# Weight blocks fetched two products ahead, and three second norms one product sooner, in a four-stage layer chain on one core

## The chip, the cores and the metric

The kernel runs on one core of one Trainium2 chip. The metric is device time in microseconds (us) of one execution; the numbers below are medians of several executions. Everything is float32. In the profile PE is the matmul engine, PEld its weight load, DVE the vector engine, ACT the activation engine, POOL the GpSimd engine and SP the engine that issues most transfers. The profile writes two records for each matmul of this kernel, so "x16" is eight matmuls.

## The reference

Input x has 4 batches of 1024 tokens with 1024 features. Four stages follow each other, each closed by a residual sum and a layer norm without weights:

```python
x = _layernorm(x + _L0_attn_ref(x, weight, mask))       # x @ (weight * block mask).T
x = _layernorm(x + _L0_ffn_ref(x, ...))                 # x @ W.T + bias, + a LoRA term for some batches
x = _layernorm(x + _L1_attn_ref(x, ...))                # the sequence model, below
x = _layernorm(x + _L1_ffn_ref(x, ...))                 # x @ W.T + b, + 8 routed LoRA experts per batch
```

The sequence model projects 1024 features to 128, runs four layers, and projects back to 1024. One layer on h (tokens by 128):

```python
y = silu(layernorm(h, l1w, l1b))       # the first norm
y = sconv(y, ...)                      # a complex first-order recurrence along the tokens, real part
h = h + y * scl                        # the linear part
y = layernorm(h, l2w, l2b)             # the second norm
y = silu(y @ w1.T + b1) @ w2.T + b2    # 128 -> 512 -> 128
h = h + y
```

## The kernel before, in words

**Units and products.** The 4096 tokens are 8 units of 512 (two for each batch). Each unit goes through stage 0 (masked attention weight), stage 1 (LoRA layer) and later stage 3. The batch's own sequence model (stage 2) is woven in between products of other units. Features lie on the 128 partitions. Stages 0 and 1 use a Strassen scheme with seven half-size products, in two halves of the output, so `project` runs 14 products (p, i) for a stage: `weight(p, i)` gives the operand, eight matmuls of 128x256 into one of four PSUM banks (`mm`), an eviction on DVE (z<-mm,z) or, for i = 0, on ACT, and then `tick()`. One product with its pieces is one tick of a clock.

**The blocks.** From unit 1 on, the seven combined weight blocks come from device memory: `a0q_s` for stage 0, `a1q_s[b]` for stage 1 (one for each batch, with that batch's LoRA term merged in). `streamed(q)` returns a `weight` that takes a tile "wq" (128 x 4 x 256, 512 KB) from a pool of five buffers and issues its load on SP (L420) at that product. A load can start once PE has finished with the buffer's earlier block. `adapt1(b)` merges the LoRA weights in pieces planned at ticks around the unit before their use, and stores the blocks of `a1q_s[b]` on SP (L301). On the same queue stand the next unit's input xT (`load_x`, L472, two loads of 1 MB), reloads x<-x_s for the sequence model's way out (`leave`, L583), reloads w<-a_s for the merges (L845), the sequence model's tables ct and sn (L872) and layer weights mw (L876). SP issues its transfers in one order; each also waits until the transfer eight places earlier has landed.

**Who sets the order.** PE and DVE are reached through `InOrder` (L83 to L110), which keeps their instructions in the program's order; so all their lines show as L104 in the profile. ACT, POOL and SP instructions are ordered by the framework, from the program's order and from when it reckons that operands and buffers are ready.

**The plan.** `put(at, piece, pe, dve)` hangs a piece of side work on a tick; `tick()` runs what hangs there. `put_in` spreads pieces over a stretch, by the PE and DVE time that `put` has counted for its ticks. `later_rows` places a stage norm's sums on the first tick that isn't in `taken`, and sequence norms enter `taken` through `put_rows`.

**The sequence model.** `sequence(b, at, layer, ahead)` starts at tick 56b + 59. A batch's 1024 tokens are two halves j = 0, 1 of 512, the second 7 ticks behind the first; a layer takes 13 ticks for batches 0 to 2 (`slack` is then 1) and 12 for batch 3. For one layer l and half j, with `base` its first tick:

- base: `rows`: four small matmuls stats<-csq over the squares, a square root on ACT (sd, L243), a reciprocal on DVE, four broadcasts on POOL (L249) into crs. The tile sd has one buffer for the sequence.
- base + 1: `first`: crs<-h,crs on DVE, Silu on ACT. base + 2, base + 3: `scan`, two recurrences on DVE. base + 4: `joined`, three DVE products, result u.
- base + 5 + slack: `convolved`: one matmul cv<-u,csc on PE, h<-h,cv on DVE, the square csq<-h on ACT (L862).
- base + 7 + slack: `rows` again, for the second norm; base + 8 + slack: `normed`, crs<-h,crs on DVE.
- base + 9, 10, 11 + slack: `forward` in three steps: matmuls a_ps<-crs,mw, Silu on ACT (a_sb, L931), matmuls o<-a_sb,mw one step later, then h<-o,b2c,h on DVE and the next square.

The `a_ps` and `cv` results share two PSUM banks.

Of the kernel before, what the change touches and what calls it, by code (L numbers as in the profile page):

```python
# [17 lines left out]
P = 128  # L18
# [17 lines left out]
NU = NB * S // U  # L36
PRODUCT = 3.7
HU = U // 2
# [15 lines left out]
def block_kernel(  # L54
# [25 lines left out]
    nc = tc.nc  # L80
# [114 lines left out]
    def block(name, shape):  # L195
        return big(name, shape, "blk", 5)
# [60 lines left out]
    SLOTS0 = (0, 5, 4, 1, 6, 2, 3)  # L257
# [74 lines left out]
    def put(at, piece, pe=0.0, dve=0.0):  # L332
        plan.setdefault(at, []).append(piece)
        count(at, pe, dve)
# [77 lines left out]
        o = [t[0][:, 0], t[0][:, 1], t[1][:, 0], t[1][:, 1]]  # L412
        return o if cs is None else [a[:, cs, :] for a in o]

    def streamed(q):


        def weight(p, i):
            w = block("wq", [P, 4, HU])
            nc.sync.dma_start(w, q[SLOTS0[i], p])  # L420
            return lambda c, o: w[:, c, ds(o * P, P)]

        return weight

    def on_chip(parts):
        def weight(p, i):
# [6 lines left out]
    def project(weight, ops, z, after, early=None, order=IN_ORDER):  # L433

        for p, i in order:
            cs = ds(2 * p, 2)
            c11, c12 = z[0][:, 0, cs, :], z[0][:, 1, cs, :]
            c21, c22 = z[1][:, 0, cs, :], z[1][:, 1, cs, :]  # L440
            w = weight(p, i)
            ps = bank().rearrange("p (o n) -> p o n", n=HU)
            for o in range(2):
                product(ps[:, o, :], lambda c: w(c, o), ops[i], 4)
            if i == 0:
                A.copy(c11, ps)
            elif i == 1:
                V.tensor_tensor(c21, ps, c11, ALU.add)
            elif i == 2:
                V.tensor_tensor(c12, ps, c21, ALU.add)  # L450
            elif i == 3:
                V.tensor_tensor(c22, ps, c12, ALU.add)
                V.tensor_tensor(c21, ps, c21, ALU.add)
            elif i == 4:
                V.tensor_tensor(c12, ps, c12, ALU.add)
            elif i == 5:
                V.tensor_tensor(c11, ps, c11, ALU.add)
            else:
                V.tensor_tensor(c21, ps, c21, ALU.add)
            if early:  # L460
                early(p, i)
            add_squares()
            if i > 4:
                after(p, i - 5)
            tick()
# [31 lines left out]
    def stage0(ops):  # L497
        ssum, z, t = big("ssum", [P, U], "ssum", 2), z_tiles(), t_tiles([4, HU])
        norm = {}

        def after(p, j):
            for c in range(2 * p, 2 * p + 2):
                square_in(z[j][:, :, c, :], None, ssum, p == 0 and j == 0 and c == 0)

        def early(p, i):
            cs = ds(2 * p, 2)
            lo, hi = ([z[j][:, h, cs, :] for h in range(2)] for j in range(2))
            for k in {4: (3,), 5: (1, 2), 6: (4,)}.get(i, ()):
                right_sum(k, lo, hi, t_out(t, cs))

        project(streamed(a0q_s), ops, z, after, early)
        later_rows(1, lambda: norm.update(rs=norm_rows(ssum)))
        return mixed(z, t), norm

# [334 lines left out]
    def sequence(b, at, layer, ahead):  # L849


        st = {}

        def h_of(j):
            return hs[b][:, ds(j * HF, HF)]

        def t_tile(name):
            return big(name, [P, HF], "t", 4)

        def square(j):  # L860
            st[j, "sq"] = sq = t_tile("csq")
            A.activation(sq, h_of(j), AF.Square)  # L862

        def rows(j):
            sd, seg = rstd_rows(st[j, "sq"], HF, avg_c, "sc")
            st[j, "y"] = rs = t_tile("crs")
            spread(rs, sd, seg)

        def tables_in(l, j):
            for k, (name, src) in enumerate((("ct", ct_s), ("sn", sn_s))):  # L870
                st[j, k] = t = big(name, [P, HF], name, 2)
                nc.sync.dma_start(t, src[l][:, ds(j * HF, HF)])  # L872

        def weights_in(l):
            st["mw"] = big("mw", [P, 2 * DFF], "mw", 1)
            nc.sync.dma_start(st["mw"], mw_s[l])  # L876

        def normed(j):
            y = st[j, "y"]
            V.tensor_tensor(y, h_of(j), y, ALU.mult)  # L880

        def first(l, j):
            normed(j)
            y = st[j, "y"]
            A.activation(y, y, AF.Silu, bias=col("ln1_b", l), scale=col("ln1_w", l))

        def scan(l, j, k):

            y = st[j, "y"]
            out = y if k else t_tile("u")  # L890
            V.tensor_tensor(out, st[j, k], y, ALU.mult)
            start = (g1i, g2i)[k][:, l : l + 1] if j == 0 else st["end", k]
            V.tensor_tensor_scan(
                out, rad[:, l : l + 1].to_broadcast([P, HF]), out, start, ALU.mult, ALU.add
            )
            if j == 0:
                st["end", k] = end = small.tile([P, 1], F32, name="end", tag=f"end{k}")
                A.copy(end, out[:, HF - 1 : HF])
            st[j, "out", k] = out

        def joined(j):
            u, y = st[j, "out", 0], st[j, "out", 1]
            V.tensor_tensor(u, st[j, 0], u, ALU.mult)
            V.tensor_tensor(y, st[j, 1], y, ALU.mult)
            V.tensor_tensor(u, u, y, ALU.add)

        def convolved(l, j):
            cv = spot("cv")
            T.matmul(cv, lhsT=csc[:, l, :], rhs=st[j, "out", 0], start=True, stop=True)
            V.tensor_tensor(h_of(j), h_of(j), cv, ALU.add)  # L910
            square(j)

        def forward(l, j, step):

            if step == 0:
                st["o"] = accp.tile([P, HF], F32, name="o2", tag="o2")
            for f in range(2 * step - 2, 2 * step):
                if f >= 0:
                    T.matmul(
                        st["o"], lhsT=st["mw"][:, ds(DFF + f * DIM, DIM)], rhs=st[f, "a"],  # L920
                        start=(f == 0), stop=(f == FC - 1),
                    )
            for f in range(2 * step, 2 * step + 2):
                if f < FC:
                    a = spot("a_ps")
                    T.matmul(
                        a, lhsT=st["mw"][:, ds(f * P, P)], rhs=st[j, "y"],
                        start=True, stop=True,
                    )
                    st[f, "a"] = s = big("a_sb", [P, HF], "a_sb", 4)  # L930
                    A.activation(s, a, AF.Silu, bias=b1c[:, l * FC + f : l * FC + f + 1])  # L931
            if step == 2:
                h = h_of(j)
                V.scalar_tensor_tensor(h, st["o"], b2c[:, l : l + 1], h, ALU.add, ALU.add)
                square(j)

        def final(j):
            V.tensor_tensor(h_of(j), h_of(j), st[j, "y"], ALU.mult)

        def put_rows(k, j):  # L940
            put(k, partial(rows, j), 0.9, 0.95)
            taken.add(k)

        slack = layer > SHORT
        for j in range(2):
            put(at + ahead * j - 1, partial(square, j))
        for l in range(DEPTH):
            for j in range(2):
                base = at + layer * l + ahead * j
                put(base - 2, partial(tables_in, l, j))  # L950
                put_rows(base, j)
                if j == 0:
                    put(base + ahead, partial(weights_in, l))
                put(base + 1, partial(first, l, j), 0.0, 0.7)
                put(base + 2, partial(scan, l, j, 0), 0.0, 1.9)
                put(base + 3, partial(scan, l, j, 1), 0.0, 1.9)
                put(base + 4, partial(joined, j), 0.0, 2.1)
                put(base + 5 + slack, partial(convolved, l, j), 0.9, 0.7)
                put_rows(base + 7 + slack, j)
                put(base + 8 + slack, partial(normed, j), 0.0, 0.7)  # L960
                put(base + 9 + slack, partial(forward, l, j, 0), 1.8, 0.0)
                put(base + 10 + slack, partial(forward, l, j, 1), 3.5, 0.0)
                put(base + 11 + slack, partial(forward, l, j, 2), 1.8, 0.75)
        for j in range(2):
            base = at + layer * DEPTH + ahead * j
            put_rows(base, j)
            put(base + 1, partial(final, j), 0.0, 0.7)
# [425 lines left out]
        put(15 + 2 * c, partial(operands0, c), 0.0, 2.8)  # L1393

    def enter(g, ops, rs):
        stage1(g, ops, rs, streamed(a1q_s[g // 2]))


    def mw_prep(l):
# [356 lines left out]
```

## Time and profile before

| what | value |
|---|---|
| median of 3 runs | 1709.11 us (1708.22 to 1710.04) |
| the profiled execution | 1708.12 us |
| its span, first to last instruction | 1706.4 us |
| mean granted TensorE clock | 0.997 |
| PE busy | 1678.1 us |
| DVE busy | 1284.9 us |
| ACT busy | 627.5 us |
| transfers, mean | 232 GB/s |

PE's matmuls are recorded in a pipeline and their ends are modelled, so a row of PE that is x16 and 3.62 long is one product of eight matmuls. The costliest groups of the page (busy time, mean ns of one, idle time just before them and what ended most of it) show what PE does:

```profile
L104 PE MATMUL mm<-tt,wq 128*128 128x256 f32 x1792 | 407.7, 381 | 0.0
L104 PE MATMUL mm<-z,wq 128*128 128x256 f32 x672 | 152.2, 380 | 2.7 <-DMA wq<-a1q_s 2.7
```

The first row reads the products that take sums of inputs, the second those that take a stage's results directly; the second has waited 2.7 us in all for blocks of stage 1.

### The profile page before, as it was taken

How to read it: one execution, taken by the hardware profiler on the slowest of the kernel's cores; microseconds unless marked ns; L12 is line 12 of the kernel's file. 1: busy time of each engine (PE TensorE's matmuls, PEld its weight loads, DVE VectorE, ACT ScalarE, POOL GpSimd, SP SyncE). 2: the span in 40 equal slices, each digit the busy share in tenths (PEclk: the TensorE clock that was granted, in tenths of full speed). 3: DMA queues.
4: the chain of work that ended last, by engine and by line, in shares of the span. 5: the costliest groups of instructions: out<-in, count | busy, mean ns of one | idle time of the engine just before them, and what ended most of it. 6: DMA issues, size and time to landing. Idle time of an engine off the chain costs nothing.

```text
span 1706.4 us, 19199 instructions
## 1 busy us (share of the span) xinstructions
PE 1678.1 (98%) x6345; PEld 1043.0 (61%) x6345; DVE 1284.9 (75%) x2173; ACT 627.5 (37%) x1079; POOL 220.3 (13%) x454
## 2 busy tenths in 40 slices
PE   7999999999999999999999999999999999999998
PEld 3488887767677666666766676765444444444444
DVE  5799889677567879767887887777778878676743
ACT  4411112355343245443333444423344642333012
POOL 1110111221011012101120111101111200100000
PEclk9999999999999999999999999999999999999999
DMA  9967879956745985576889558696536737964211
GB/s 373 367 229 268 276 259 368 358 197 222 259 136 180 324 294 172 172 284 213 297 287 340 180 167 282 223 303 211 176 111 220 227 118 246 354 221 143 94 67 62
DMA packets 194709, 395.90 MB, mean 232 GB/s; under 512 B 16657, under 2 KB 105889, under 8 KB 189874
## 3 DMA queue, kind: packets, MB, share of 16 engines
q1 hardware_dynamic: 187602, 371.82, 63.4%
q0 software_dynamic: 6048, 21.37, 3.3%
q10 hardware_dynamic: 960, 1.48, 0.2%
q8 instruction: 50, 0.82, 0.2%
q14 instruction: 49, 0.40, 0.1%
HBM read 268.39 MB, written 126.23 MB: 231 GB/s over the span
## 4 chain that ended last, share of the span: by engine, by line
PE 72%; DVE 5%; DMA 2%; ACT 0%; issue 0%; SPq 0%; POOL 0%; ACTq 0%; DVEq 0%
PE mm L104 57%; PE o L104 6%; PE a_ps L104 6%; PE stats L104 2%; DMA a1q_s<-s 1%; DVE z L104 1%; PE cv L104 1%; DVE x L104 1%; DMA wq<-a1q_s 1%; DVE u L104 1%; DVE crs L104 0%; DVE tt L104 0%; DVE w L104 0%; DVE s L104 0%; DVE ssum L104 0%
## 5 line engine op out<-in xcount | busy, mean ns | idle before, releaser
L104 PE MATMUL mm<-tt,wq 128*128 128x256 f32 x1792 | 407.7, 381 | 0.0
L104 DVE TENSOR_TENSOR z<-mm,z 128x512 f32<-128x512 f32 x339 | 226.7, 684 | 231.3 <-PE mm L104 229.8
L104 PEld LDWEIGHTS mm<-tt,wq 128*128 128x128 f32 x1792 | 337.2, 190 | 75.0 <-issue 23.7
L249 POOL PARTITION_BROADCAST crs<-sd x288 | 139.9, 595 | 825.8 <-DVE sd L104 632.0
L104 PE MATMUL mm<-w3q,x 128*128 128x512 f32 x384 | 173.0, 596 | 0.0
L104 PE MATMUL mm<-z,wq 128*128 128x256 f32 x672 | 152.2, 380 | 2.7 <-DMA wq<-a1q_s 2.7
L104 PE MATMUL mm<-xT,wq 128*128 128x256 f32 x672 | 153.1, 382 | 0.0
L104 PEld LDWEIGHTS mm<-z,wq 128*128 128x128 f32 x672 | 127.1, 190 | 33.0 <-issue 12.5
L104 PEld LDWEIGHTS mm<-xT,wq 128*128 128x128 f32 x672 | 126.1, 190 | 26.0 <-issue 6.1
L104 PE MATMUL mm<-w3q,s 128*128 128x512 f32 x288 | 130.4, 596 | 0.0
L104 PE MATMUL a_ps<-crs,mw 128*128 128x512 f32 x256 | 122.4, 601 | 5.6 <-DVE crs L104 5.6
L104 PEld LDWEIGHTS mm<-w3q,x 128*128 128x128 f32 x384 | 71.9, 190 | 88.2 <-issue 87.7
L931 ACT ACTIVATE a_sb<-a_ps,b1c 128x512 f32<-128x512 f32 x128 | 86.3, 684 | 105.0 <-PE a_ps L104 104.6
L104 DVE TENSOR_TENSOR ssum<-ssum,sq 128x512 f32<-128x512 f32 x168 | 115.5, 688 | 11.7 <-ACT sq L391 5.1
L104 DVE RECIPROCAL sd<-sd 128x128 f32<-128x128 f32 x96 | 91.1, 949 | 41.4 <-ACT sd L243 40.1
L104 PE MATMUL o<-a_sb,mw 128*128 128x512 f32 x256 | 120.3, 592 | 0.0
L691 ACT ACTIVATE sq<-z 128x512 f32<-128x512 f32 (+1 forms) x65 | 40.5, 624 | 157.4 <-DVE z L104 144.4
L104 DVE TENSOR_TENSOR w<-w,mm 128x512 f32<-128x512 f32 x128 | 81.5, 679 | 17.7 <-PE mm L104 14.2
L104 PEld LDWEIGHTS mm<-w3q,s 128*128 128x128 f32 x288 | 53.8, 190 | 65.4 <-issue 64.5
L104 PE MATMUL mm<-b,aT 16*128 16x512 f32 (+1 forms) x256 | 87.7, 620 | 0.1
L104 PEld LDWEIGHTS a_ps<-crs,mw 128*128 128x128 f32 x256 | 48.6, 192 | 59.9 <-issue 50.3
L243 ACT ACTIVATE sd<-stats,eps 128x128 f32<-128x128 f32 x96 | 35.3, 367 | 125.8 <-PE stats L104 97.2
(248 smaller groups left out, 2136.4 us busy)
## 6 DMA issues: line engine op xcount, KB each, us to landing
wq<-a0q_s SPq DMA_DIRECT2D x98, 512.0 KB, 3.4
wq<-a1q_s SPq DMA_DIRECT2D x98, 512.0 KB, 5.8
w<-a_s SPq DMA_DIRECT2D x48, 512.0 KB, 5.8
w3q<-a3q_s SPq DMA_DIRECT2D x21, 1024.0 KB, 9.8
a1q_s<-w SPq DMA_DIRECT2D x64, 256.0 KB, 3.8
x_s<-z SPq DMA_DIRECT2D x16, 1024.0 KB, 6.7
x<-x_s SPq DMA_DIRECT2D x64, 256.0 KB, 6.5
x_s<-x SPq DMA_DIRECT2D x128, 128.0 KB, 2.6
```

The costliest lines, as they stand in the source:

```text
L104: ins = op(*args, **kw)
L243: A.activation(sd[:, :seg], ps[:, :seg], AF.Sqrt, bias=eps)
L249: G.partition_broadcast(dst[:, ds(j * seg, seg)], sd[32 * j : 32 * j + 1, :seg], channels=P)
L691: A.activation(sq[:, cols], z[:, m, ds(n * HF, HF)][:, cols], AF.Square, accum_out=st[:, m, n : n + 1] if out is None else out,)
L931: A.activation(s, a, AF.Silu, bias=b1c[:, l * FC + f : l * FC + f + 1])
```

## The change

Two things, in the same functions.

First, `streamed` is no longer made for one stage. A generator lists all blocks of units 1 to 7 in order of use (stage 0's, then stage 1's, for each unit), and every call of `streamed(p, i)` issues loads until three blocks are in flight or in use (`FETCH = 2`), and then hands out the oldest. So a block's load is put into the program two products ahead of its product, also across the border between stages and units. The pool still has five buffers.

Second, for three layers (batch 0 layer 0, batch 1 layer 1, batch 2 layer 1), in the second half of the tokens, `convolved`, the second `rows` and `normed` hang one tick earlier. `forward` stays where it was.

```diff
-    def streamed(q):
-
-
-        def weight(p, i):
-            w = block("wq", [P, 4, HU])
-            nc.sync.dma_start(w, q[SLOTS0[i], p])
-            return lambda c, o: w[:, c, ds(o * P, P)]
-
-        return weight
+    FETCH = 2
+    fetched = []
+
+    def to_fetch():
+        for g in range(1, NU):
+            for q in (a0q_s, a1q_s[g // 2]):
+                for p, i in IN_ORDER:
+                    yield q[SLOTS0[i], p]
+
+    coming = to_fetch()
+
+    def streamed(p, i):
+
+        while len(fetched) <= FETCH:
+            src = next(coming, None)
+            if src is None:
+                break
+            fetched.append(block("wq", [P, 4, HU]))
+            nc.sync.dma_start(fetched[-1], src)
+        w = fetched.pop(0)
+        return lambda c, o: w[:, c, ds(o * P, P)]
...
-        project(streamed(a0q_s), ops, z, after, early)
+        project(streamed, ops, z, after, early)
...
-                put(base + 5 + slack, partial(convolved, l, j), 0.9, 0.7)
-                put_rows(base + 7 + slack, j)
-                put(base + 8 + slack, partial(normed, j), 0.0, 0.7)
+                early = slack and (b, l, j) in ((0, 0, 1), (1, 1, 1), (2, 1, 1))
+                put(base + 5 + slack - early, partial(convolved, l, j), 0.9, 0.7)
+                put_rows(base + 7 + slack - early, j)
+                put(base + 8 + slack - early, partial(normed, j), 0.0, 0.7)
...
-        stage1(g, ops, rs, streamed(a1q_s[g // 2]))
+        stage1(g, ops, rs, streamed)
```

In the program as built, PE, DVE, POOL and SP have the same number of instructions before and after, and ACT has two table loads fewer.

## The prediction

> **What bounds the kernel now.** I read the page's totals first, then the waits of PE, then the timelines around each wait, and last the chain of waits and SP's queue before them.
>
> ```profile
> PE 1678.1 (98%) x6345; PEld 1043.0 (61%) x6345; DVE 1284.9 (75%) x2173; ACT 627.5 (37%) x1079; POOL 220.3 (13%) x454
> ```
>
> PE is busy for 1678.1 of 1706.4 us, so only its idle time, about 28 us, and matmuls that run slow can be won. The waits of PE (total, times, longest) say who causes the idle time; the rest of it lies mostly at the start and the end.
>
> ```profile
> PE stats L104 <- DVE rows L104: 9.7, 2, 7.0
> PE a_ps L104 <- DVE crs L104: 5.6, 4, 2.8
> PE mm L104 <- DMA wq<-a1q_s: 2.7, 2, 2.3
> ```
>
> The change touches the second and third lines: a_ps, the first FFN matmul of a sequence layer, waiting for the normed tile crs; and stage 1's products, waiting for a weight block. PE's timeline (start, duration, idle before, releaser):
>
> ```profile
> 347.84 3.40 PE L104 MATMUL a_ps<-crs,mw 128*128 128x512 f32 x4 [2.77 <-DVE crs L104]
> 354.53 1.88 PE L104 MATMUL o<-a_sb,mw 128*128 128x512 f32 x4
> 607.81 3.69 PE L104 MATMUL mm<-z,wq 128*128 128x256 f32 x16 [0.35 <-DMA wq<-a1q_s]
> 716.53 1.98 PE L104 MATMUL a_ps<-crs,mw 128*128 128x512 f32 x4 [1.27 <-DVE crs L104]
> 735.02 0.42 PE L104 MATMUL stats<-csq,avg_c 128*32 128x128 f32 x8
> 927.98 3.69 PE L104 MATMUL mm<-z,wq 128*128 128x256 f32 x16 [2.35 <-DMA wq<-a1q_s]
> 1036.71 1.98 PE L104 MATMUL a_ps<-crs,mw 128*128 128x512 f32 x4 [1.27 <-DVE crs L104]
> ```
>
> The reader sees five places. 347.84 is batch 0, layer 0, second half; 716.53 and 1036.71 are batches 1 and 2, layer 1, second half: just the three that the change names. The four matmuls at 347.84 also take 3.40 instead of 1.98: in the table by stretches the granted clock is 0.58 from 347.8 to 351.3 and 1.00 from 351.3 on. Behind the 2.35 wait at 927.98 it is 1.00.
>
> **The sum's own time.** The profiled execution took 1708.12 (span 1706.4 and 1.72 around it), 0.99 below the median of 1709.11. Savings are worked out in that execution and taken off the median. PE's losses below are the times from start to start less the usual spacing of that kind of matmul, so they lie slightly above the gaps printed.
>
> **Part 1: second norm one product sooner, batch 0.** The loss here is 2.93 of waiting and 1.43 of matmuls at the low clock, 4.36 together. Why crs is late:
>
> ```profile
> 339.35 1.28 ACT L243 ACT_TABLE_LOAD   x1
> ```
> ```profile
> 341.05 0.95 DVE L104 RECIPROCAL sd<-sd 128x128 f32<-128x128 f32 x1 [1.97 <-ACT sd L243]
> 361.69 0.69 DVE L104 TENSOR_TENSOR z<-mm,z 128x512 f32<-128x512 f32 x1 [4.88 <-PE mm L104]
> ```
> ```profile
> 342.15 3.46 POOL L249 PARTITION_BROADCAST crs<-sd  x4 [4.40 <-PE mm L104]
> 336.50 1.26 POOL L249 PARTITION_BROADCAST crs<-sd  x4
> ```
>
> The sums end on PE at about 337.9; ACT is in a Silu and a table load until 340.6, the root ends at 341.0, the reciprocal at 342.0, four broadcasts at 345.6, the product crs<-h,crs (0.69, started at 347.10 behind two stage operations) at 347.8. In the new built order cv stands directly behind the preceding `o` matmuls (about 325.1; its operand u is ready at 319.3, so no new wait), and the four sum matmuls stand one product, 3.6, sooner (about 333.9). Two table loads fall away on ACT. Then POOL decides: it is held until 335.7 by an earlier transfer's landing and does the first half's broadcasts until 337.8; the shared small tile sd comes free only then. Root to 338.3, reciprocal to 339.4, broadcasts 1.26 (to 340.7) or, beside DVE's long operations, 3.46 (to 342.9), crs by 341.4 or 343.6. PE arrives at 344.9: the wait is gone either way, by 1.3 at least. The low clock goes with it.
>
> What is late next: the Silu results for `o`. In the new order ACT has the adapter's merge (L1229, L222) and the squares ahead of the second and third Silu; I work out their ends at about 350.4 and 352.3, while PE would want them at 350.1 and 351.0. That is a new wait of about 1.4. Net 4.36 − 1.4 = 3.0; bounds 1.0 (3.4 of new waiting: ACT's 1.28 table load and its three neighbours of 0.7 in front) and 4.36 (none). It is kept to the end: behind this place DVE idles 4.88 waiting for PE (361.69 above), so nothing there takes it back.
>
> By the Trainium skill, "TensorE: Matmul & The Clock Gate", Part 1, the array falls to half rate after an idle window of some 3.4 us. The wait here was shorter, so by the page the low clock isn't owed to it (rival D below). The row says otherwise (2.77 idle, then 0.58), and I go by the row.
>
> **Part 2: the same, batches 1 and 2.** PE's loss is 1.43 each (gap 1.27). The new crs comes at about 709.7, PE at 715.1: this wait goes. But what does PE meet next? DVE waits for PE at 707.84, and from there to 734.9 its lines leave no gap; the first and the last of them:
>
> ```profile
> 707.84 1.29 DVE L104 TENSOR_TENSOR z<-mm,z 128x512 f32<-128x512 f32 x2 [1.85 <-PE mm L104]
> ...
> 733.56 0.75 DVE L104 SCALAR_TENSOR_TENSOR h<-o,b2c,h 128x512 f32<-128x512 f32 x1
> 734.22 0.68 DVE L104 TENSOR_TENSOR h<-h,cv 128x512 f32<-128x512 f32 x1
> ```
>
> stats<-csq at 735.02 follows them through ACT's square with no printed wait. The new order has the same DVE operations in that stretch (two reciprocals of 0.95 change places, two x<-x,boutc,rs go later in it), so the chain ends where it did, and PE, 1.43 earlier, waits there. Net 0 each (bounds −0.25, a stage norm's sums and broadcasts one product later, to +1.43). Batch 2 is the same pattern, to 1055.
>
> **Part 3: blocks put into the queue two products ahead.** Most of it moves nothing: the built order of SP is the same over most of the program, because five buffers already let each load stand as early as PE frees its buffer. It differs at about seven stage boundaries, where a stage's first blocks now go ahead of the next unit's input xT, and of some stores and reloads. Only two of these have a PE wait today:
>
> ```profile
> 905.32 7.47 DMA a1q_s<-s
> 912.80 8.19 DMA a1q_s<-s
> 921.62 6.22 DMA wq<-a1q_s
> ```
>
> This is the chain of waits into 927.98: SP lets a transfer start only when the eighth before it has landed, so the block's load stands behind stores of the merged weight. In the new order the first block takes xT's place (910.7 instead of 921.6; at the other boundary 591.4 instead of 602.1), ahead of those stores. With the slowest landing in this stretch, 8.3, it is there at 919 and 600, and PE asks at 925.5 and 607.3: margins above 6. Losses 2.51 and 0.52 go, 3.03 in all (bounds 0 and 3.03). What waits behind it on SP: the last stores, four reloads x<-x_s, the second block, and xT's second half (issued some 12 later, landing about 932, first read after 940). The second block waits for a store's landing (about 921–922) and lands 7.05 later, at 929; PE, now earlier, asks at 934.2: margin about 5. At the other boundaries, and for the shifted reloads of tables and of w (one or two places), PE has no wait and consumers are 5 or more away: 0.
>
> **Sum.** 3.0 + 0 + 0.52 + 2.51 = 6.0 saved: 1708.12 − 6.0 = 1702.1 in the profiled execution, 1709.11 − 6.0 = **1703.1** as a median.
>
> **Rivals.** 0.2% is 3.42 us, about what a measurement of this kernel can tell from no change; "same" is 1705.7 to 1712.5.
> - A: DVE isn't the bound at 735 and 1055, so batches 1 and 2 keep 1.43 each: 6.0 + 2.86 gives 1700.2. For it: just before 707.84 DVE still has 1.85 to spare. Against: the 27 us without a gap behind it.
> - B: one of the two main gains fails. Either the first block stays late (its buffer or the stores hold it), 1706.1, for which the 8 us landings speak; or ACT's order eats batch 0's gain to 1.0, 1705.1, for which its 3.38 busy of 3.5 there speaks. Both together: 1709.11 − 1.0 = 1708.1.
> - C, slower: the second block holds SP. It stands at the queue's head until a store has landed, with everything behind it. If that landing and the load grew from 15.3 by more than the margin of 5 at both boundaries, PE would stand there; from about 3.0 per boundary beyond the margin the whole gain is gone, and at 5 beyond (landings near 13 each) the time is 1709.11 − 6.0 + 10 = 1713.1. For it: DMA's share is 0.97 to 1.03 from 925 to 932. Against: the bytes are the same, and a 1 MB load leaves the front of the stores.
> - D: the slow matmuls at 347.84 aren't owed to the wait, and their 1.43 stays: 1704.5. Against: both come and go together in the only two long waits shown (2.77 with, 2.35 without, which puts the threshold between them).
>
> **How the numbers follow.** Forecast 0.52 (its own range 1701.7 to 1705.1, from the new ACT wait of 0 to 3.4), A 0.16, B 0.19, C 0.09, D 0.04. Of B 0.04 lies at 1705.1, in "faster", and 0.15 in "same"; so faster is 0.52 + 0.16 + 0.04 + 0.04 = 0.76, same 0.15, slower 0.09. The range leaves out C and the edge of A and B: 1699.0 to 1709.0.
>
> **What would show it.** Right: the a_ps wait on crs shrinks from 5.6 to under 0.6 with no clock below 0.9 near 348; the wait on wq<-a1q_s vanishes; a wait of 1 to 2 appears at `o` near 350 on ACT's a_sb, and one of about 1.3 at stats<-csq where 735.02 was. Wrong: PE waits on a1q_s blocks again (the second block above all), on xT, or on z evictions behind a reordered DVE.

## The result and the profile after

The changed kernel took 1703.45 us in the median of six executions (1702.47 to 1706.05), against 1709.57 for the kernel before beside it: a ratio of 0.9965 with a 95% interval of 0.9952 to 0.9977. Run again later beside other kernels, it took 1704.43 in the median of eleven against 1708.80: 0.9974 (0.9965 to 0.9983). So it is faster by 4 to 6 us.

The profiled execution took 1704.36, with a span of 1702.6 and these waits of PE (total, times, longest):

```profile
PE stats L104 <- DVE rows L104: 9.8, 2, 7.1
PE stats L104 <- ACT csq L874: 3.4, 2, 1.7
PE stats L104 <- DVE bcol L104: 1.4, 1, 1.4
...
PE o L104 <- ACT a_sb L943: 0.9, 2, 0.7
PE a_ps L104 <- DVE crs L104: 0.3, 1, 0.3
```

The two waits that the prediction named have gone: a_ps on crs has fallen from 5.6 to 0.3, and that on wq<-a1q_s isn't in the list any more. Two new ones stand in their place, o on a_sb and stats on csq. PE's timeline at the five places (start, duration, idle before, releaser):

```profile
347.09 1.88 PE L104 MATMUL a_ps<-crs,mw 128*128 128x512 f32 x4
348.81 3.62 PE L104 MATMUL mm<-z,wq 128*128 128x256 f32 x16
352.66 1.13 PE L104 MATMUL o<-a_sb,mw 128*128 128x512 f32 x2 [0.23 <-ACT a_sb L943]
354.46 1.12 PE L104 MATMUL o<-a_sb,mw 128*128 128x512 f32 x2 [0.67 <-ACT a_sb L943]
...
606.45 3.62 PE L104 MATMUL mm<-z,wq 128*128 128x256 f32 x16
...
713.66 1.88 PE L104 MATMUL a_ps<-crs,mw 128*128 128x512 f32 x4
733.61 0.42 PE L104 MATMUL stats<-csq,avg_c 128*32 128x128 f32 x8 [1.70 <-ACT csq L874]
...
924.06 3.62 PE L104 MATMUL mm<-z,wq 128*128 128x256 f32 x16
...
1031.28 1.88 PE L104 MATMUL a_ps<-crs,mw 128*128 128x512 f32 x4
1051.23 0.43 PE L104 MATMUL stats<-csq,avg_c 128*32 128x128 f32 x8 [1.70 <-ACT csq L874]
```

And SP's, ahead of the place at 924 (start, duration, transfer):

```profile
908.93 0.33 SPq L433 DMA_DIRECT2D wq<-a1q_s  x1
909.70 0.36 SPq L301 DMA_DIRECT2D a1q_s<-s  x1
910.37 0.36 SPq L301 DMA_DIRECT2D a1q_s<-w  x1
911.19 1.15 SPq L301 DMA_DIRECT2D a1q_s<-s  x2
912.39 1.56 SPq L595 DMA_DIRECT2D x<-x_s  x2
916.89 0.34 SPq L433 DMA_DIRECT2D wq<-a1q_s  x1
```

The first block is now issued 15 us ahead of its product, in front of the last stores; the second 7 us ahead of that same product. Before the change the first was issued 6.4 ahead of it (921.62, for 927.98).

**How the runs are read.** The span is only 3.8 us shorter than before, while the medians differ by 6.1. The difference lies ahead of 262 us, where both kernels run the same matmuls. Take the matmul stats<-csq that starts at 262.01 in the kernel before and at 264.20 in the changed one: up to it the new profile has lost 2.19, and from it to the end of the span it takes 1438.45 instead of 1444.40, 5.95 less. Most of that loss, 1.68, is one product that takes 5.40 instead of 3.72, in the following stretch with a granted clock of 0.53 (view by stretches; the columns behind the stretch's length are the busy times of PE, PEld, DVE, ACT and POOL, then the clock, the DMA share and GB/s):

```profile
core 0: us, PE busy (x) PEld busy (x) DVE busy (x) ACT busy (x) POOL busy (x), PEclk, DMA share, GB/s
251.00:252.80 1.80, 0.43 (x8) 0.35 (x8) 1.72 (x4) 0.00 (x0) 0.00 (x0) 1.00 0.90 351
252.90:256.50 3.60, 3.60 (x16) 2.78 (x13) 2.75 (x4) 0.37 (x1) 1.66 (x3) 0.53 0.72 199
```

It follows a wait of 1.37 on bcol at 251 that the kernel before has too, there at a clock of 1.00. So below each kernel has two numbers: its median, and its profile's time "from 262 on", which leaves this first part out.

| kernel | median (executions) | before, beside it | ratio (95% interval) | from 262 on |
|---|---|---|---|---|
| before | 1709.57 (6) | | | 1444.40 |
| the change | 1703.45 (6) | 1709.57 | 0.9965 (0.9952 to 0.9977) | 1438.45 |
| the change, again | 1704.43 (11) | 1708.80 | 0.9974 (0.9965 to 0.9983) | 1441.15 |
| loads ahead alone | 1708.15 (11) | 1708.37 | 0.9997 (0.9989 to 1.0006) | 1441.24 |
| the same, again | 1708.41 (10) | 1707.60 | 1.0000 (0.9990 to 1.0009) | 1440.54 |
| the same, third | 1707.12 (11) | 1708.80 | 0.9991 (0.9981 to 1.0002) | 1441.08 |
| early norms alone | 1704.82 (12) | 1708.37 | 0.9980 (0.9971 to 0.9988) | 1440.35 |
| loads, batch 0's norm | 1702.80 (6) | 1707.60 | 0.9969 (0.9957 to 0.9981) | 1438.22 |
| change, one piece later | 1702.55 (8) | 1708.37 | 0.9970 (0.9960 to 0.9981) | 1438.42 |
| one piece later, batch 0's norm | 1700.48 (5) | 1708.37 | 0.9953 (0.9940 to 0.9966) | 1436.07 |
| change, weight preparation later | 1700.41 (6) | 1707.60 | 0.9960 (0.9948 to 0.9972) | 1436.46 |
| both later, batch 0's norm | 1700.26 (6) | 1707.60 | 0.9957 (0.9945 to 0.9970) | 1433.78 |
| change, one product ahead | 1703.24 (9) | 1708.86 | 0.9973 (0.9963 to 0.9983) | 1436.87 |
| both later, output weight later | 1697.56 (5) | 1708.86 | 0.9934 (0.9920 to 0.9947) | (other order there) |

### The profile page after: what moved, and what is told of

Same layout as the page of the kernel before. It is cut to its first block, busy times and chain, and to the rows that moved or that the text cites. A ratio compares the mean times of both kernels' runs of the same rounds, so it can differ in the third digit from the quotient of the medians.

```text
span 1702.6 us, 19199 instructions
## 1 busy us (share of the span) xinstructions
PE 1677.8 (99%) x6345; PEld 1043.9 (61%) x6345; DVE 1284.6 (75%) x2173; ACT 623.9 (37%) x1077; POOL 216.4 (13%) x454
## 4 chain that ended last, share of the span: by engine, by line
PE 89%; DVE 6%; issue 3%; DMA 1%; ACT 1%; POOL 0%; ACTq 0%; DVEq 0%; POOLq 0%
PE mm L104 73%; PE o L104 6%; PE a_ps L104 6%; PE stats L104 2%; PE cv L104 2%; DVE z L104 1%; DVE x L104 1%; DVE w L104 1%; DVE u L104 1%; DVE crs L104 1%; DVE ssum L104 1%; DMA lo_s<-b_raw 0%; DMA b<-lo_s,pick 0%; DMA lo_s<-aT 0%; DVE tt L104 0%
## 5 line engine op out<-in xcount | busy, mean ns | idle before, releaser
L249 POOL PARTITION_BROADCAST crs<-sd x288 | 134.3, 576 | 812.7 <-DVE sd L104 623.5
```

The lines of the kernel that those rows point to most:

```text
L249: G.partition_broadcast(dst[:, ds(j * seg, seg)], sd[32 * j : 32 * j + 1, :seg], channels=P)
```

## The experiments

### The loads ahead alone

```diff
-                early = slack and (b, l, j) in ((0, 0, 1), (1, 1, 1), (2, 1, 1))
+                early = 0
```

> Only the loads two products ahead; the three norms stay where they were. Theory (the terms of the sum add up, and the two halves of the change don't touch each other): the waits of stage 1's products on a1q_s blocks vanish, 2.5 at about 926 and 0.5 at about 607; the waits of a_ps on crs stay at 2.8, 1.3 and 1.3, and with the first of them the slow matmuls at about 348. 3.0 us faster than before, ratio 0.9982. Rival (the blocks were hidden anyway, or are late for another reason): the waits on wq<-a1q_s stay above 2, ratio 1.000.

The waits on a1q_s blocks are gone, as the theory had it, and from 262 on the profile is 3.2 shorter. But the median of the executions is hardly below before. PE's timeline of its first profile at batch 0's first layer:

```profile
348.66 1.98 PE L104 MATMUL a_ps<-crs,mw 128*128 128x512 f32 x4 [3.23 <-DVE crs L104]
350.48 3.62 PE L104 MATMUL mm<-z,wq 128*128 128x256 f32 x16
```

The wait is longer than before the change (3.23 against 2.77), and the four matmuls behind it take 1.98, not 3.40: no half rate here. So a second profile:

> The loads ahead alone, once more, for a second profile. Its first profile shows the waits on blocks gone and a span 2.8 shorter, but the median of its executions was only 0.2 below before, with a spread of 6. Theory (a half-rate stretch of PE, worth about 1.8, follows some waits in some executions and not in others; this kernel keeps the waits of 3.2, 1.3, 1.3 and 1.4): the profile of a slow execution has one or more such stretches behind a wait, and span less stretches and waits is that of the first profile within 0.5. Rival (an execution is slow for a transfer that is late): a slow execution shows longer waits on blocks or tables.

This profile fell on an execution of 1710.86, 5.5 slower than the first one. All of that lies ahead of 262: the matmul there starts at 268.61 instead of 262.36, and from 262 on the second is even 0.7 shorter. In that first part there is a wait of 1.50 before 60.86, and three stretches at half clock, where the first profile has one (at 67.27). The first stands behind that wait, the last near 258 behind the wait on bcol, as in the changed kernel. The second follows no wait:

```profile
62.70:66.11 3.41, 3.41 (x5) 1.35 (x4) 2.23 (x7) 2.72 (x6) 1.39 (x2) 0.50 0.44 179
76.36:79.76 3.40, 3.33 (x8) 1.16 (x8) 3.33 (x6) 0.15 (x1) 0.00 (x0) 1.00 0.90 316
79.77:83.18 3.41, 3.41 (x5) 1.33 (x4) 3.41 (x7) 0.00 (x0) 0.00 (x0) 0.50 0.98 344
```

From 76.36 to 79.76 PE is busy for 3.33, mostly with the matmuls mm<-b,aT, which use 16 of the array's 128 rows; every profile has one stretch of this kind, starting between 66 and 80. No transfer is late after 262. So the theory holds for two of the three stretches. The longer waits on blocks or tables that the rival had named don't show; what ended the wait of 1.50 stays open (the profile names no engine and no transfer). To see whether the changed kernel has the same luck, both ran once more side by side.

> The loads ahead alone, third time. Theory (what it lost in the median before was chance in the part ahead of 262 us, where its program is that of the changed kernel): from 262 on 1440.5 to 1441.3, and its median 2.1 to 2.9 above that of the changed kernel run beside it, ratio to before about 0.998. Rival (it has a loss of its own that the changed kernel doesn't have): its median stays 4 or more above the changed kernel's, ratio 1.000, and the profile shows the loss in a place after 262 or a longer first part again.

> The changed kernel once more, beside the loads-ahead-alone kernel on the same chip. From 262 us on its profile takes 1438.4 within 0.5, as its first profile did; the part before 262 is left to chance between 261.9 and 268.6. Median 1703.5, ratio to before 0.9965.

The loads alone came out 2.7 above the changed kernel, as the theory said, but only 1.7 below before, at a ratio of 0.9991 and not 0.998. From 262 on they have given 3.2, 3.9 and 3.3. Over three sittings (32 executions), though, their medians lie only 0.2 below, 0.8 above and 1.7 below before's. The mean granted clock of each execution shows why. At 0.998 or 0.999 the loads are faster: 9 executions have a median of 1705.23, against 1707.44 in 19 of the kernel before. But 18 of the 32 ran at 0.996 or less, against 18 of 76 of the kernel before (and 1 of 17 of the changed kernel), and there both have a median of 1709.3. So the loads gain, and lose most of it again to more time at half clock. Where these executions have their stretches, and why the reordered loads bring more of them, stays open: none at 0.996 or less has a profile.

The changed kernel's second profile missed its number, 1441.15 instead of 1438.4, and the median came out at 1704.43 instead of 1703.5. The place is batch 0's new wait:

```profile
353.46 1.12 PE L104 MATMUL o<-a_sb,mw 128*128 128x512 f32 x2 [1.46 <-ACT a_sb L943]
355.26 1.65 PE L104 MATMUL o<-a_sb,mw 128*128 128x512 f32 x2 [0.67 <-ACT a_sb L943]
```
```profile
355.30:358.80 3.50, 3.50 (x5) 1.61 (x6) 3.36 (x5) 1.67 (x3) 0.57 (x1) 0.56 0.79 246
```

It is longer (1.46 and 0.67 instead of 0.23 and 0.67), and behind it the clock falls to 0.56, which costs another 1.7. In this execution batch 0's early norm has gained only 0.1.

Why the wait is longer shows on POOL, which is held by the landing of its own load ahead of its broadcasts (the first profile of the change, then the second):

```profile
337.95 0.99 POOL L249 PARTITION_BROADCAST rs<-sd  x3 [5.84 <-DMA b<-lo_s,pick]
338.76 0.98 POOL L249 PARTITION_BROADCAST rs<-sd  x3 [6.45 <-DMA b<-lo_s,pick]
```

Counted from the matmul at 262 (264.20 and 263.76 in these two), POOL goes on 73.75 behind it in the first and 75.00 in the second, 1.25 later. DVE's next reciprocal, ACT's first Silu result and the first `o` each start 1.24 later. So the size of this wait follows one landing.

### The early norms alone

The edit is the second part of the change on the kernel before.

> Only the three second norms one product sooner; loads as before. Theory: batch 0 gains 4.4 and loses 1.2 to a new wait of o on a_sb, batches 1 and 2 gain 1.4 each and lose it again at the next stats<-csq (waits of about 1.7 there); the waits on a1q_s blocks stay (0.4 and 2.4). 3.1 us faster than before, ratio 0.9982. Rival (batches 1 and 2 keep their gain): no wait at stats<-csq, 6.0 faster, ratio 0.9965.

1704.82, ratio 0.9980: 3.5 below before, close to the theory's 3.1. The two waits at stats<-csq are there with 1.7 each, so batches 1 and 2 don't keep their gain. One thing was not expected: the wait on blocks fell from 2.7 to 1.6 though no load was moved (at the second boundary from 2.35 to 0.90; at the first it grew from 0.35 to 0.71). In the chain of waits the stores and the load at the second boundary landed faster in this execution (7.42, 7.34 and 6.07, against 7.47, 8.19 and 6.22 before). These landings account for 1.05 of the 1.45 by which the wait is shorter, so what fetching ahead can win at this boundary hangs on them. How much they vary in one and the same kernel, two profiles of two kernels can't tell.

### Only batch 0's norm early

```diff
-                early = slack and (b, l, j) in ((0, 0, 1), (1, 1, 1), (2, 1, 1))
+                early = slack and (b, l, j) == (0, 0, 1)
```

> The whole change without the early norms of batches 1 and 2. Theory (those two gain nothing, since DVE and then ACT end the next step): the two waits of a_ps on crs are back at 1.3, the two at stats<-csq are gone from the list, and the time is that of the changed kernel, 1703.5, ratio to before 0.9965. Rival (they gain): 2.8 slower than the changed kernel, 1706.3, ratio 0.998.

From 262 on 1438.22 against 1438.45, and a median not above the change's. Matched by the same matmuls, each of the two places without its early norm comes out within 0.04 of the change. Two of the change's three early norms are worth nothing.

### A piece of x<-x,boutc,rs later

The four pieces hang on four ticks in the stretch between a_ps and the next stats<-csq, for the way out of the batch before. The last of the four places moves behind h<-h,cv.

```diff
-            put_in(
-                last + 4 + k, min(last + 8, gate - 2),
-                places(*((("leave", 2 * b + k), j) for j in range(4))), 0.0, 1.4,
-            )
+            parts = places(*((("leave", 2 * b + k), j) for j in range(4)))
+            behind = parts[3:] if k == 1 and b < 2 else []
+            put_in(last + 4 + k, min(last + 8, gate - 2), parts[: 4 - len(behind)], 0.0, 1.4)
+            for piece in behind:
+                put(gate - 2, piece, 0.0, 1.4)
```

> The whole change, and one of the four pieces of x<-x,boutc,rs (two DVE instructions of 0.7 each) moved behind h<-h,cv for batches 0 and 1 on their way out, which run in the stretches of the early norms of batches 1 and 2. Theory (DVE is the bound from the a_ps matmuls to the next stats<-csq): 1.4 us less of DVE work stands ahead of the square, so each of the two waits at stats<-csq falls from 1.7 to about 0.3, and the time by 2.8 against the changed kernel: 1700.7, ratio to before 0.9948. Rival (another cause ends the square, ACT or PE's own order): both waits stay at 1.7 and the time is that of the changed kernel, ratio 0.9965.

> As e3, but only batch 0's norm is early; batches 1 and 2 wait for crs as before the change. Theory: DVE reaches the square 1.4 sooner, but PE now loses 1.4 at each a_ps, so neither alone gives anything: 1703.5, ratio 0.9965, as the changed kernel; with e3 this shows that the early norms of batches 1 and 2 are worth 1.4 each once DVE is relieved, and nothing before. Rival (the moved piece is worth 1.4 by itself at each place): 1700.7, ratio 0.9948, as e3.

Both expectations missed, in opposite ways. With all three norms early, the waits at stats<-csq are gone altogether, so DVE was what ended there. But another took their place 12 us sooner, and nothing was won:

```profile
717.96 1.02 PE L104 MATMUL o<-a_sb,mw 128*128 128x512 f32 x2
720.42 1.13 PE L104 MATMUL o<-a_sb,mw 128*128 128x512 f32 x2 [1.44 <-ACT a_sb L943]
732.67 0.43 PE L104 MATMUL stats<-csq,avg_c 128*32 128x128 f32 x8
```

ACT had three squares of x (L626) and two operations on z (L388, L391) between the two Silu results. With batch 0's norm early only, the same moved piece gave the rival's time, in a way that neither had named: no wait at a_ps, none at o, none at stats<-csq.

```profile
712.86 1.98 PE L104 MATMUL a_ps<-crs,mw 128*128 128x512 f32 x4
714.68 3.62 PE L104 MATMUL mm<-tt,wq 128*128 128x256 f32 x16
718.14 1.88 PE L104 MATMUL o<-a_sb,mw 128*128 128x512 f32 x4
...
731.35 0.43 PE L104 MATMUL stats<-csq,avg_c 128*32 128x128 f32 x8
```

DVE's timeline says why:

```profile
709.46 1.42 DVE L104 SCALAR_TENSOR_TENSOR x<-x,boutc,rs 128x512 f32<-128x512 f32 x2
710.80 0.68 DVE L104 TENSOR_TENSOR z<-mm,z 128x512 f32<-128x512 f32 x1
711.51 0.69 DVE L104 TENSOR_TENSOR tt<-z,z 128x512 f32<-128x512 f32 x1
712.12 0.69 DVE L104 TENSOR_TENSOR crs<-h,crs 128x512 f32<-128x512 f32 x1
```

Moving one piece has shifted the others by a tick, and only two of these instructions are left ahead of crs<-h,crs where the kernel before had four (2.78):

```profile
711.77 2.78 DVE L104 SCALAR_TENSOR_TENSOR x<-x,boutc,rs 128x512 f32<-128x512 f32 x4
```

So crs is ready 1.4 sooner with the norm where it was. The same relief serves the a_ps wait and the chain to stats<-csq; the expectation had counted it for the second only. From 262 on this is 2.4 below the change: 1.4 at each of the two places, less 0.6 by which batch 0's wait for a_sb was longer in this profile. It needs neither of the two early norms.

### The third weight's first chunk later

```diff
-            put(74 + 5 * c + i, partial(total, i), 0.0, 0.3)
-            put(75 + 5 * c + i, partial(centre, i), 0.0, 0.2)
+            put(74 + 5 * c + i + 4 * (c == 0), partial(total, i), 0.0, 0.3)
+            put(75 + 5 * c + i + 4 * (c == 0), partial(centre, i), 0.0, 0.2)
```

> The whole change, and the first chunk of the third weight's preparation (on ACT two sums of 1.1 and two subtractions of 1.15, L222 and L1242, on DVE four short operations) four products later, away from batch 0's first feed-forward matmuls. Theory (the Silu results a_sb wait behind these on ACT): the two waits of o on a_sb at about 352 to 354 (0.2 and 0.7 in the profile, 1.2 from start to start) go, 1.2 faster than the changed kernel, ratio to before 0.9958. Rival (a_sb is late for the matmuls' or another engine's sake): the waits stay.

The waits of o on a_sb are gone:

```profile
344.82 1.88 PE L104 MATMUL a_ps<-crs,mw 128*128 128x512 f32 x4
346.53 3.62 PE L104 MATMUL mm<-z,wq 128*128 128x256 f32 x16
349.99 1.88 PE L104 MATMUL o<-a_sb,mw 128*128 128x512 f32 x4
```

From 262 on it is 2.0 below the change's first profile, and the median 1700.41. Of the 2.0, 1.44 are won at this place; the rest is a shorter wait for the output weight's load near 1495, which lies between none and 0.7 in these profiles. The preparation on ACT was the cause.

### The pieces together, and one wait more

The edits are the moved piece, batch 0's norm early only, and the third weight's first chunk later, all as above.

> The loads ahead, batch 0's early norm, the piece of x<-x,boutc,rs moved behind, and the third weight's first chunk four products later. If the terms add: the 1700.5 of the third and fourth of these kernels' better one, less 1.2 for the waits of o on a_sb: 1699.3, ratio to before 0.9946. If the moved chunk collides with the second one, a new wait of stats or a_ps appears near 365 to 380 and the time stays at 1700.5.

The terms add in the profile (1433.78 from 262 on, 2.3 below the better of the two before it); the median, 1700.26 with executions from 1697.45 to 1702.34, doesn't show it. In the first part the wait on bcol at 251 is still there. The next kernel moves the output weight's preparation from 2 ticks ahead of its old rhythm to 1:

```diff
-        put(39 + 5 * n - 2 * (n == DEPTH), work)
+        put(39 + 5 * n - (n == DEPTH), work)
```

> The kernel with both pieces later, and the output weight's preparation one product later, so that its sums don't stand on PE and DVE ahead of a stage norm's sums at about 251. Theory: the wait of stats on bcol (1.4, in every execution) goes, and with it the half-rate stretch of 1.8 that follows it in some executions; 1.4 faster in the profile and a little more in the median: about 1698.5, ratio to before 0.994. Rival (the half-rate stretch near 253 doesn't hang on that wait): it still shows up in some executions, and the spread stays. Or the wait only moves to the next tick's sums: no gain.

The wait at 251 is gone, and the executions lie between 1697.13 and 1699.37: this version beats both kernels, at 0.9934 of before. The profile doesn't show the 1.4 that was expected: its execution took 1698.69, 1.2 more than the profiled one of the kernel with both pieces later. Two new waits are together longer than the one that went, one of 0.49 at 261 and this one:

```profile
295.85 2.43 PE L104 MATMUL mm<-tt,wq 128*128 128x256 f32 x10 [1.62 <-ACT h L575]
```

ACT stands there behind the landing of b_raw<-in_b_dram, so whether this wait comes with the edit, one profile can't tell. What the median has won goes with the clock: 4 of these 5 executions ran at 0.998 or more, 2 of the 6 with both pieces later.

### One product ahead instead of two

The edit is FETCH = 1.

> The whole change with the loads put in one product ahead instead of two (FETCH = 1). In the built order the first block of stage 1 still stands ahead of xT's second half and of the last stores, the second block behind xT. Theory (only the first block was late; five buffers cover the rest): no wait on a1q_s blocks, and from 262 us on the same time as the changed kernel, 1438.4 within 0.5. Rival (the second block needs its place too): a wait of 1 or more at the second product of stage 1, about 615 or 933.

No wait on blocks at either boundary: the second block needs no place further ahead, and the depth of two isn't what helps. The time from 262 on, 1436.87, lies 1.6 below the change, outside the expected 0.5, mostly (1.2) because o waits for a_sb only 0.3 in this profile. ACT's order there is the change's; POOL goes on 72.58 behind the matmul at 262 (262.66 there), 1.17 sooner than in the change's first profile, and the wait is shorter by as much.

## Why the prediction was right, and where it was not

The forecast was 1703.1, measured 1703.45 and, later, 1704.43. That the first median came so close was in part luck: the second sitting saved 4.4 and not 6.0, and the first profiled execution took 1704.36, where the sum had 1702.1 for it, mostly because a half-rate stretch fell on its first part. Step by step, by starts of the same matmuls behind each place, before and after (a row that had waited is also some 0.1 longer, which the prediction's losses leave out):

| step | said | first profile | second profile |
|---|---|---|---|
| batch 0, a_ps comes sooner | −4.36 | −4.46 | −4.46 |
| batch 0, new wait of o on a_sb | +1.4 | +1.44 | +2.67, and 1.70 of half rate behind it |
| batches 1 and 2, each | −1.43 + 1.43 | −1.54 + 1.56 | −1.54 + 1.56 |
| first blocks at 607 and 928 | −3.03 | −3.18 | −3.19 |
| output weight's load, near 1497 | 0 | +0.20 | −0.08 |
| sum said; measured from 262 on | −6.0 | −5.95 | −3.25 |

**Batch 0.** Right in its mechanism and, for the first profile, its size. ACT's order was read well: the wait came at the named matmul, and moving the named pieces away removed it. Wrong was the bound: "bounds 1.0 (3.4 of new waiting...) and 4.36", with "the low clock goes with it". In the second profile the wait cost 2.67 and was followed by a half-rate stretch, and the net was 0.1, below the lower bound. The bound came from ACT's work alone. The landing that holds POOL, which the prediction had read as 335.7 from the kernel before (73.7 behind the matmul at 262), was taken as fixed; in the first profile it came out the same (73.75), so the 1.4 fitted, and in the second it was 1.25 later. That is rival B's second case, batch 0's gain eaten, by a cause that B had not named.

**Batches 1 and 2.** Right: a wait is not gone when the next one on the same chain comes from an engine that has no gap. DVE's 27 us without a gap told it, and rival A is excluded by the kernel without these two norms. The reason was only half told: relieving DVE brought up ACT next (with the norms early) or nothing (with them late).

**The blocks.** Right in place and size, but the 2.51 is the loss of one execution; the only other profile without the loads moved showed a wait of 0.9 at the same place. And in the medians the loads alone have not won it, since they ran at half clock more often. Rival C, the second block holding the queue, was far off: it was issued at 916.89 and PE never waited for it.

**The clock.** Here the prediction's row was misread. It took 2.77 idle with a clock of 0.58 behind it, and 2.35 idle with 1.00, for a threshold on the length of a wait, and rival D's argument rested on it. A wait of 3.23 with no low clock behind it (loads alone, above) and one of 1.37 with a low clock (the change, at 251) refute that. Rival D itself did not come true: the matmuls at 347.09 take 1.88, at a clock of 1.00 from 346.5 to 352. What counts is how much of a wait falls into one window of the clock, as the last section shows, and that differs from one execution to the next. The range of 1699.0 to 1709.0 covered this scatter only because other uncertainties had made it wide.

## What to carry to other kernels

Where a wait is to be removed, read what the engine in front of it does until the next place where the same engines meet: if that stretch has no gap, the wait will only move, and taking work out of the stretch helps where moving the waiting chain doesn't. Before crediting a change by its median, align the two traces by the same instructions and see where the time went; here a part in which PE's matmuls are the same before and after scattered by more than the change was worth. Where a term of the sum hangs on one landing, take it for a range: batch 0's wait followed that landing almost to the hundredth. And of several edits that travel together, try each alone: one of the three early norms and the first block's place did all of it.

## What was not expected of the hardware

A stretch at half clock, costing 1.4 to 1.7, follows some PE waits in some executions. Which ones, the stretches by clock show (the kernel before, the loads alone in their first profile, the change in its first):

```profile
343.91:347.31 3.40, 1.16 (x6) 0.68 (x4) 3.37 (x5) 1.43 (x4) 1.70 (x3) 1.00 0.46 135
347.32:350.73 3.41, 2.89 (x4) 1.34 (x5) 3.37 (x7) 3.29 (x6) 0.00 (x0) 0.50 0.15 62
...
343.75:347.16 3.41, 1.68 (x8) 1.14 (x6) 3.38 (x5) 1.18 (x3) 2.69 (x3) 1.00 0.48 154
347.16:350.57 3.41, 1.91 (x5) 0.95 (x6) 3.37 (x6) 2.68 (x5) 0.00 (x0) 1.00 0.29 109
...
249.73:253.14 3.41, 2.04 (x22) 1.66 (x20) 2.98 (x6) 0.00 (x0) 0.00 (x0) 1.00 0.92 361
253.14:256.55 3.41, 3.41 (x12) 2.79 (x9) 2.80 (x4) 0.37 (x1) 1.71 (x3) 0.50 0.73 197
```

In all profiles each such stretch inside the program is 3.41 long at a clock of 0.50, and the starts of two in one execution lie whole multiples of 3.413 apart (67.43 and 347.32 in the kernel before: 82 of them; 75.65 and 253.14 in the change: 52). So in these traces the clock changes on a grid of 3.41, and half rate comes behind a window of this grid in which PE has done little. The wait of 2.77 had 2.25 in one window, one of 2.55 (the third profile of the loads alone) 2.08: half rate. That of 3.23 was split into 1.73 and 1.50, one of 3.10 (the second profile) into 1.17 and 1.93: none. The wait of 1.37 at 251 lay whole in one window in 3 of the 13 profiles that have it, and in just these half rate followed; in the other ten no window had more than 1.16 of it. Of 25 waits of 0.7 to 2.4 from 604 on, none had more than 1.95 in one window, and behind none stood half rate. The place of the grid differs from one execution to the next, and so does what follows the same wait.

An exact bound stays open, and it isn't idle time alone: at 251 the same window also holds 0.95 of matmuls with one moving column, from 76 to 80 in the second profile of the loads alone the matmuls on 16 rows were enough with hardly any wait, and behind the wait at 353 in the second profile of the change 1.82 in one window was enough.

By the Trainium skill, "TensorE: Matmul & The Clock Gate", Part 1, the clock falls to half after an idle window of about 3.4 us, and the window runs freely, so that the place of a matmul in it matters. The grid of 3.413 and its shifting place agree with that, and an estimate from the page, one window at half rate or 1.7 us, agrees with the 1.4 to 1.7 measured; that the window must be idle does not agree, for PE was busy for 1.16 of the 3.40 ahead of 347.32.
